# A gated cross-attention and expert kernel: the passage from its first to its second phase rewritten (gates of three tiles on TensorE, twenty slot buffers, loads from one queue)

## The chip, the cores and the metric

The kernel runs on one core of a Trainium2 chip. A core has four engines that compute, each with its own instruction stream executed in order: TensorE (PE, matrix products), VectorE (DVE), ScalarE (ACT) and GpSimd (POOL). SyncE (SP) computes nothing; it issues DMA transfers. ACT and POOL can issue them too, and an engine that has to wait before it issues one holds up everything queued behind it. The metric is the device time of one execution in microseconds (us), as a median of several executions; lower is better.

## The reference

Two gated residual blocks over x of shape (4, 2048, 512), all in float32. The first is cross-attention with 16 heads of 64 to a context of 77 rows per batch; the second is a mixture of 8 experts with a gate over 10 choices (two of them "null"), top 2.

```python
x = x + tanh(g_xattn) * xattn(layernorm(x), ctx, ...)     # attention: q, k, v, softmax, w_out, b_out, tanh(gate)
x = x + tanh(g_ffn)   * ffn(layernorm(x), ...)

def ffn(inputs, gate_w, gate_b, expert_w, expert_b):      # per token
    gate_probs = softmax(x @ gate_w.T + gate_b)           # 10 choices
    weights, selected = top_k(gate_probs, 2)
    true_weights = weights * (selected < 8)
    norm_w = true_weights / denom                         # denom: their sum, or 1
    return sum_k norm_w[k] * (x @ expert_w[selected[k]] + expert_b[selected[k]])
```

## The kernel before

The 8192 tokens are 64 tiles of 128. **Phase 1** goes over the tiles in a software pipeline written out by hand in `step(i)` (line 673): one step computes the attention scores of tile i+1, `attend` (L360: the product of the transposed attention with the folded value and output weights, 20 matmuls) of tile i-1, the residual and the second layer norm of tile i-1, and the gate logits of tile i-2. `attn_move` (L353) turns the attention of a tile by 16 small DMAs from SP. A normed tile is left in one of nine row buffers `rows` (dictionary `hrs`).

The gate logits of a tile (`gate_logits`, L382) are ten products-with-sum on VectorE, one for each choice, against `gwb`, a copy of the gate weights on every partition. `choose` (L410 to L424) takes the two largest, `ratio` (L430) their exponential on ACT, `weigh` (L440 to L445) the weights of the two choices, `place` (L453, TensorE) the running counts, and `dispatch` (L463 to L475) the row numbers, after which POOL scatters the 128 rows to two DRAM arrays `hb[0]` (first choices) and `hb[1]` (second choices), sorted by expert. `place` and `dispatch` take two tiles at a time (m = tile // 2).

**Phase 2** goes over 118 slots of 128 rows, listed in `order`: 16 full blocks that are known early, 35 known after the last tile, 8 partly filled ones, all of first choices; then 51 full and 8 partly filled ones of second choices. A slot n has six parts:

- `slot_load` (L902, L905) reads the start row from a table into a register (L892) and loads the block by five DMAs into a buffer of `ring`. Slots up to 8 are loaded by SP alone; later ones have three of the five DMAs on SP and two on ACT. Partly filled slots are gathered by POOL instead (L881).
- `slot_acc` (L925): POOL gathers the same tokens' rows of the output so far.
- `slot_tr` (L943): the block is transposed on VectorE (partly filled slots: by ACT and TensorE, L952 to L958).
- `slot_pe` (L981): eight matmuls with the expert's weights, into one of six PSUM buffers (`px` and `pe` in turn).
- `slot_out` (L989, L990): VectorE adds the bias, scales, and adds the gathered row.
- `slot_put` (L997): POOL scatters the result to the output.

`first_table`, `second_table` and `part_table` (L831 to L863, VectorE) compute the tables of the slots that depend on all counts.

What sets the order is the program's own text: it is emitted under a manual schedule, so each engine executes its share in the order in which the functions are called. The passage between the phases (L1106 to L1161) is written out: after the last `step`, slots 0 and 1 are multiplied, then tiles 62 and 63 are attended, with the gate logits of 61 and 62 in between and those of 63 spread over the first slots by `tail(q)`. The loop over q from 1 to 118 then runs loads 5 ahead, gathers 3 ahead and transposes 2 ahead. `ring` has 11 buffers: row buffers and pieces of the attention buffers. A load into a buffer waits until the slot that held it has been put.

On the hardware queues of SP and ACT together the program uses eight completion semaphores in rotation: each transfer waits, before it is issued, for the transfer eight before it.

Of the kernel before, what the change touches and what calls it, by code (L numbers as in the profile page):

```python
# [18 lines left out]
P = 128  # L19
# [5 lines left out]
def kernel(  # L25
# [351 lines left out]
    def gate_logits(i, e0, e1):  # L377
        if e0 == 0:
            pgs[i] = stile("pg", i, NG)
        for e in range(e0, e1):  # L380
# [10 lines left out]
            )  # L391


    csum = [small.tile([P, 2, 2, NG], BF16, tag="cs", name="cs_init")]
# [53 lines left out]

    def place(m):

        pps[m] = pp = mm_tile(f"pp{m}")
        for n, (w, v) in enumerate(((upper, msks[m]), (ones_b, counted.pop(m)))):
            nc.tensor.matmul(  # L453
                pp[:, : 4 * NG],
                w,
                v.rearrange("p t k e -> p (t k e)"),
                start=(n == 0),
                stop=(n == 1),
            )

    def dispatch(m):
        pos, pp = poss.pop(m), pps.pop(m)
        nc.vector.tensor_tensor(  # L463
            pos[:, :, :, :NG],
            pp[:, : 4 * NG].rearrange("p (t k e) -> p t k e", t=2, k=2),
            msks.pop(m),
            ALU.mult,
        )
        dst = small.tile([P, 2, 2], I32, tag="dst", name=f"dst_{m}")
        with nc.allow_low_precision("row numbers are whole and below 2^24"):  # L470
            nc.vector.tensor_reduce(dst, pos, AX.X, ALU.add)
        for i in (2 * m, 2 * m + 1):
            hr = hrs.pop(i)
            for k in range(2):
                ins = nc.gpsimd.indirect_dma_start(  # L475
                    out=hb[k],
                    out_offset=bass.IndirectOffsetOnAxis(ap=dst[:, i % 2, k : k + 1], axis=0),
                    in_=hr[:, :].bitcast(I32),
                    in_offset=None,
                    bounds_check=NROWS - 1,  # L480
                    oob_is_err=False,
                )
                tc.declare_no_dep(ins.ins, group="scatter", reason="rows of one bucket differ")
                tc.add_to_no_dep_group("scatter", ins.ins)
                if i > SNAP:
                    tc.declare_no_dep(ins.ins, group="block", reason="blocks full by tile SNAP")
                    tc.add_to_no_dep_group(f"late{i}", ins.ins)

# [184 lines left out]
    def step(i):  # L673
# [14 lines left out]
        if i == NT - 2:  # L688
            slot_tr(0)
            slot_tr(1)  # L690
        if is_tile(i - 1):
# [81 lines left out]
    ]  # L773
    scr = m_flat[:, 6 * D :]
    assert NT * (2 * NE + 1) <= NC * COLS - 6 * D

    def count_rows(cs):
        pc = mm_tile("pc")
# [91 lines left out]
    ]  # L870
    ring += rows[NRB - 3 : NRB - 1]
    px_pool = []
    hss, metas, toks, accs, hsTs, exps, pes, turn = {}, {}, {}, {}, {}, {}, {}, [0, 0]

    def slot_load(n):
# [13 lines left out]
        else:  # L889
            both = n > N1 // 2  # L890
            queues = (nc.sync, nc.scalar) if both else (nc.sync,)
            r = nc.values_load(  # L892
                starts[t][0:1, s : s + 1],
                engines=[ENG.SP, ENG.Activation] if both else [ENG.SP],
                min_val=0,
# [5 lines left out]

            loads = [queues[0].dma_start(hs[:, D:].bitcast(I32), block[:, D:])]  # L902
            for g in range(4):
                loads.append(
                    queues[g // 2 * (len(queues) - 1)].dma_start(  # L905
                        hs[g * 32 : (g + 1) * 32, :D]
                        .rearrange("p (j d) -> p j d", j=4)
                        .bitcast(I32),
                        block[:, g * P : (g + 1) * P].rearrange("(j a) d -> a j d", a=32),
                    )  # L910
                )
# [25 lines left out]
    def slot_tr(n):  # L937
# [11 lines left out]
        ptr = tr_tile(f"str{n}")  # L949
        hp, hsT = (hTs[(turn[1] + k) % len(hTs)] for k in range(2))  # L950
        turn[1] += 2
        nc.scalar.copy(  # L952
# [8 lines left out]
    def slot_pe(n):  # L961
# [13 lines left out]
        hsT = hsTs.pop(n)  # L975
        if n % 2:
            pe = mm_tile(f"pe{n}")
        else:
            pe = px_pool[0].tile([P, 512], F32, tag="px", name=f"px{n}")
# [41 lines left out]
    def rest():  # L1021
# [7 lines left out]
        with tc.If(count > EVER * P):  # L1029
            for n in range(M, len(order)):  # L1030
                for part in (slot_load, slot_acc, slot_tr, slot_pe, slot_out, slot_put):
                    part(n)

    def tail(q):

        i = NT - 1
        if q < 5:
            gate_logits(i, 2 * q, 2 * q + 2)
        elif q == 5:
            choose(i)  # L1040
            ratio(i)
        elif q == 8:
            weigh(i // 2)
            place(i // 2)
            pc = count_rows(csum[0][:, 0])
            dispatch(i // 2)
            first_table(pc)
        elif q == 12:
            second_table()
        elif q == 14:  # L1050
            part_table()

    with tc.manual_schedule():
# [50 lines left out]
        attn_move(1)  # L1104
        nc.sync.dma_start(gwb, gate_w.partition_broadcast(P))
        for i in range(1, NT - 1):  # L1106
            if i == SNAP + 3:
                whole(full[:, 0, :], count_rows(csum[0][:, 0])[:, 0, :])
            if i == NT - 2:
                slot_load(3)  # L1110
                slot_load(4)
            step(i)
            if i == SNAP + 3:
                early_table()
                for n in range(3):
                    slot_load(n)

        phase1.close()
        px_pool.append(ctx.enter_context(tc.tile_pool(name="ps_x", bufs=3, space=PSUM)))
        slot_load(5)  # L1120
        slot_pe(0)
        slot_pe(1)
        slot_tr(2)
        slot_tr(3)
        for i in (NT - 2, NT - 1):
            gate_logits(i - 1, 0, NG)
            attend(i)
            choose(i - 1)
            ratio(i - 1)
            residual(i)  # L1130
            norm_stats(f"h{i}", x1s[i])
            norm_root(f"h{i}")
            if i == NT - 2:
                weigh(i // 2 - 1)
                place(i // 2 - 1)
                dispatch(i // 2 - 1)
            norm_shift(f"h{i}")
            hrs[i] = rows[i % NRB]
            norm_apply(f"h{i}", hrs[i][:, :D], x1s.pop(i))
            if i == NT - 2:  # L1140
                slot_pe(2)
                slot_load(6)
        for n in range(4):
            slot_acc(n)
        tail(0)
        slot_out(0)
        for q in range(1, M + 1):
            if 1 < q < M - 5:
                slot_load(q + 5)
            slot_put(q - 1)  # L1150

            for p in range(max(q, 4), min(q + 4, M)):
                if q == max(p - 3, half if p >= half else 0):
                    slot_acc(p)
# [40 lines left out]
```

## Time and profile before

| | us |
|---|---|
| median of 4 runs (lowest to highest) | 1678.76 (1677.23 to 1681.14) |
| the profiled execution: its own time / its span | 1678.93 / 1677.1 |
| PE busy over the span | 1635.8 (98%) |
| DVE busy | 1293.0 (77%) |
| ACT busy | 884.1 (53%) |
| POOL busy | 469.0 (28%) |
| a slot's eight matmuls when nothing waits | 3.43 |
| `attend` of a tile | 8.6 |

The page cuts the span into 40 slices of 41.9 us; phase 1 ends in the 30th (about 1220 us) and the passage lies in the 30th and 31st. A timeline row gives start, duration, engine, line, what is written and read, and in brackets how long the engine had been idle and whom it waited for. A window row gives a stretch, its length, and busy time with number of instructions for each engine, then the granted clock of TensorE, the DMA share and GB/s. A row of waits gives who waited for whom, the total, how often, and the longest.

### The profile page before, as it was taken

What the parts mean: (1) busy time and instruction counts of PE and PEld (TensorE: products, weight loads), DVE (VectorE), ACT (ScalarE), POOL (GpSimd) and SP (SyncE); (2) the same over time, 40 slices, a digit from 0 to 9 for tenths busy, and PEclk for the clock granted to TensorE, in tenths of its full rate; (3) what the DMA queues carried; (4) which work ended last, traced back from release to release, by engine and by line L of the source; (5) the groups of instructions that cost most, each with busy time, mean ns of one, the idle gap of its engine ahead of it and who ended that gap; (6) DMA issues with size and microseconds to landing.
All of it is one profiled execution on the core that took longest, in us unless ns stands there. A gap on an engine that the chain in (4) does not pass through costs nothing.

```text
span 1677.1 us, 23173 instructions
## 1 busy us (share of the span) xinstructions
PE 1635.8 (98%) x4530; PEld 809.1 (48%) x4530; DVE 1293.0 (77%) x3324; ACT 884.1 (53%) x3188; POOL 469.0 (28%) x617
## 2 busy tenths in 40 slices
PE   8898999999999999999999999999988999999997
PEld 6544445454554545545454554545433444444443
DVE  1554899889898998989989899998988755466653
ACT  2454677767777777777777677776630000100001
POOL 4031111112111111112111121111217656565565
PEclk9999999999999999999999999999998999999999
DMA  7468444336533345534433566766447986688862
GB/s 236 176 195 219 113 93 93 87 96 167 155 86 85 101 100 140 157 88 108 94 94 88 151 167 143 168 139 161 108 109 236 270 239 188 174 252 233 233 188 80
DMA packets 484935, 252.07 MB, mean 150 GB/s; under 512 B 369510, under 2 KB 425830, under 8 KB 484530
## 3 DMA queue, kind: packets, MB, share of 16 engines
q1 hardware_dynamic: 423473, 134.77, 34.3%
q0 software_dynamic: 34528, 103.55, 18.8%
q10 hardware_dynamic: 26784, 12.20, 2.9%
q14 instruction: 110, 0.89, 0.2%
q8 instruction: 40, 0.66, 0.2%
HBM read 119.41 MB, written 100.52 MB: 131 GB/s over the span
## 4 chain that ended last, share of the span: by engine, by line
PE 86%; DVE 4%; DMA 3%; issue 2%; SPq 2%; ACT 1%; POOL 0%; POOLq 0%; DVEq 0%; ACTq 0%
PE po L360 30%; PE sc L281 29%; PE px L981 12%; PE pe L981 11%; DVE prod L382 2%; PE pkv L519 2%; PE xtr L261 2%; SPq L353 1%; PE pv L622 1%; DMA vw_all<-row 1%; DMA gwb<-in_L_ffn_gate_w_dram 1%; DMA acc<-out_dram,row 1%; DMA x<-in_x_dram 0%; PE pm L597 0%; PE str L957 0%
## 5 line engine op out<-in xcount | busy, mean ns | idle before, releaser
L360 PE MATMUL po<-vw,aT 128*128 128x512 f32 (+1 forms) x1280 | 562.8, 595 | 4.0 <-DVE ri L326 3.8
L281 PE MATMUL sc<-m_sb,xnT 128*128 128x385 f32 (+1 forms) x1536 | 552.9, 510 | 0.0
L382 DVE CUSTOM_DVE_ANT_0 prod<-row,gwb,gbias 128x512 f32<-128x512 f32 x640 | 478.0, 747 | 24.5 <-DMA gwb<-in_L_ffn_gate_w_dram 6.6
L360 PEld LDWEIGHTS po<-vw,aT 128*128 128x128 f32 (+1 forms) x1280 | 244.2, 191 | 307.3 <-issue 299.3
L281 PEld LDWEIGHTS sc<-m_sb,xnT 128*128 128x128 f32 x1536 | 283.9, 190 | 212.5 <-issue 86.8
L475 POOL DMA_INDIRECT hb<-row,dst x128 | 128.9, 1007 | 751.1 <-DVE nbh_h L250 672.0
L314 ACT ACTIVATE attn<-sc,nmx 128x77 f32<-128x77 f32 x1024 | 316.0, 347 | 34.4 <-DVE nmx L309 30.6
L314 ACT ACTIVATION_READ_ACCUMULATOR attn<-sc,nmx 128x1 f32 x1024 | 233.2, 228 | 0.0
L981 PE MATMUL px<-big,m_sb 128*128 (+1 forms) x472 | 213.9, 596 | 11.1 <-DVE m_sb L943 10.8
L981 PE MATMUL pe<-big,m_sb 128*128 (+1 forms) x472 | 212.5, 593 | 1.0 <-DVE m_sb L943 1.0
L981 PEld LDWEIGHTS px<-big,m_sb 128*128 128x128 f32 x472 | 89.4, 191 | 121.3 <-issue 108.4
L981 PEld LDWEIGHTS pe<-big,m_sb 128*128 128x128 f32 x472 | 88.8, 190 | 110.1 <-issue 106.9
L303 DVE TENSOR_REDUCE mx<-sc 128x5 f32<-128x385 f32 (+1 forms) x192 | 106.2, 580 | 19.5 <-PE sc L281 17.5
L233 ACT ACTIVATE sdh_h<-mvh_h,eps_t 128x1 f32<-128x1 f32 x64 | 18.9, 295 | 189.9 <-DVE rsa_a L245 180.7
L952 ACT COPY m_sb<-row 128x512 f32<-128x512 f32 x11 | 6.8, 621 | 177.1 <-DMA row<-hb,pidx 174.3
L989 DVE TENSOR_TENSOR yb<-px,blks 128x512 f32<-128x512 f32 x59 | 40.5, 686 | 76.0 <-PE px L981 74.7
L989 DVE TENSOR_TENSOR yb<-pe,blks 128x512 f32<-128x512 f32 x59 | 40.5, 687 | 76.0 <-PE pe L981 75.9
L264 ACT ACTIVATE xnT<-xtr,bet,gam 128x128 f32<-128x128 f32 x256 | 95.4, 452 | 5.3 <-PE xtr L261 5.3
L327 DVE TENSOR_TENSOR attn<-attn,ri 128x1232 f32<-128x1232 f32 x64 | 92.3, 1442 | 5.1 <-DMA aT<-attn 0.8
L373 DVE SCALAR_TENSOR_TENSOR x<-po,gx,x 128x512 f32<-128x512 f32 x64 | 48.0, 750 | 60.7 <-PE pp L453 34.6
L997 POOL DMA_INDIRECT out_dram<-acc,row x75 | 76.3, 1017 | 65.5 <-DVE acc L990 52.7
L336 DVE STREAM_TRANSPOSE attn<-attn 128x1248 f32<-128x1248 f32 x64 | 94.1, 1471 | 0.0
(163 smaller groups left out, 1540.9 us busy)
## 6 DMA issues: line engine op xcount, KB each, us to landing
aT<-attn SPq DMA_DIRECT2D x768, 40.0 KB
x<-in_x_dram SPq DMA_DIRECT2D x64, 256.0 KB
out_dram<-x SPq DMA_DIRECT2D x64, 256.0 KB
aT<-attn SPq DMA_DIRECT2D x256, 36.0 KB
row<-hb SPq DMA_DIRECT2D x138, 64.0 KB
big<-in_L_ffn_expert_w_dram SPq DMA_DIRECT2D x32, 256.0 KB
row<-hb ACTq DMA_DIRECT2D x118, 64.0 KB
vw<-vw_all SPq DMA_DIRECT2D x9, 768.0 KB
```

The source lines that it names most:

```text
L264: nc.scalar.activation(xnT[:, c, :], ptr[:, c, :], AF.Identity, bias=bet[:, c : c + 1], scale=gam[:, c : c + 1],)
L281: nc.tensor.matmul(t[:, : n1 - n0], xnTs[i][:, c, :], m_sb[:, c, n0:n1], start=(c == 0), stop=(c == NC - 1),)
L303: nc.vector.tensor_reduce(mx[:, g0:g1], scs[i, g][:, : (g1 - g0) * SK].rearrange("p (h k) -> p h k", k=SK), AX.X, ALU.max,)
L314: nc.scalar.activation(a[:, h * SK : (h + 1) * SK], t[:, k : k + SK], AF.Exp, bias=nm[:, h : h + 1], scale=SCALE, accum_out=sm[:, h : h + 1],)
L327: nc.vector.tensor_tensor(a, a, ri.unsqueeze(2).to_broadcast([P, H, SK]), ALU.mult)
L336: nc.vector.transpose(a[:, :n], a[:, :n])
L360: nc.tensor.matmul(po, aT[:m, k, :], vw[:m, k, :], start=(k == 0), stop=(k == NKC - 1),)
L382: nc.vector.tensor_tensor_reduce(prod, hrs[i][:, :D], gwb[:, e, :], 1.0, gbias[:, e : e + 1], ALU.mult, ALU.add, pgs[i][:, e : e + 1],)
L475: ins = nc.gpsimd.indirect_dma_start(out=hb[k], out_offset=bass.IndirectOffsetOnAxis(ap=dst[:, i % 2, k : k + 1], axis=0), in_=hr[:, :].bi ...
L981: nc.tensor.matmul(pe, hsT[:, c, :], w[:, c, :], start=(c == 0), stop=(c == NC - 1))
L989: nc.vector.tensor_tensor(tt, pe, b, ALU.add)
L997: ins = nc.gpsimd.indirect_dma_start(out=of, out_offset=bass.IndirectOffsetOnAxis(ap=tok, axis=0), in_=acc, in_offset=None, bounds_check=T ...
```

## The change

Five things are changed, all in the passage and in phase 2, except for a small preparation in phase 1.

1. **Gates of tiles 61, 62 and 63 on TensorE.** The gate weights are loaded once more as ten rows and transposed to `gwT` before step 4 (`setup_gate`). For the three tiles, `gate_transpose` transposes the normed tile (4 transposes, copied to SBUF by ACT), `gate_product` multiplies it with `gwT` (4 products with 10 columns, float32), and one VectorE addition adds the bias. The thirty products-with-sum on VectorE for these tiles are gone.
2. **The slots of the passage stand elsewhere.** Slot loads 3 and 4 are issued after tile 62's output instead of ahead of the last step; loads 3 to 6 stand together there, 7 to 9 after tile 63's output. Slots 1, 2 and 3 are multiplied while tiles 62 and 63 pass their gates; slots 4 and 5 around the product of tile 63's gate; `slot_out` of slots 0 and 1 stands ahead of the choice of tile 63.
3. **The scatter of the last two tiles** is issued one DMA for each of the first four values of q (`later`, `put_rows`), and the tables stand at q = 3, 6 and 9 instead of 8, 12 and 14.
4. **Twenty slot buffers, nine ahead.** `ring` gets nine pieces of `vw` more; loads run 9 ahead, transposes of full slots 4 ahead. All five DMAs of a load are on SP.
5. **Buffers.** Partly filled slots have six transposed-tile buffers of their own (in `gwb`); PSUM buffers go by threes (`n // 3 % 2`) instead of in turn.

```diff
+    def setup_gate():
+        rows10 = rows[NRB - 1][:, :D]
+        ptr = tr_tile("gwtr")
+        for c in range(NC):
+            nc.tensor.transpose(ptr[:, c, :NG], rows10[:NG, c * P : (c + 1) * P], ident[:NG, :NG])
+        nc.vector.tensor_copy(gwT, ptr[:, :, :NG])
+    def gate_transpose(i):
+        ptr = tr_tile(f"gtr{i}")
+        for c in range(NC):
+            nc.tensor.transpose(ptr[:, c, :], hrs[i][:, c * P : (c + 1) * P], ident)
+        nc.scalar.copy(hgT, ptr)
+    def gate_product(i):
+        pl = tr_tile(f"gl{i}")[:, 0, :NG]
+        for c in range(NC):
+            nc.tensor.matmul(pl, hgT[:, c, :], gwT[:, c, :], start=(c == 0), stop=(c == NC - 1))
+        pgs[i] = stile("pg", i, NG)
+        nc.vector.tensor_tensor(pgs[i], pl, gbias, ALU.add)
...
+    ring += [vw_flat[:, v * ROW : (v + 1) * ROW] for v in range(NKC * D // ROW)]
...
-            both = n > N1 // 2
-            queues = (nc.sync, nc.scalar) if both else (nc.sync,)
             r = nc.values_load(
                 starts[t][0:1, s : s + 1],
-                engines=[ENG.SP, ENG.Activation] if both else [ENG.SP],
+                engines=[ENG.SP],
...
-            loads = [queues[0].dma_start(hs[:, D:].bitcast(I32), block[:, D:])]
+            loads = [nc.sync.dma_start(hs[:, D:].bitcast(I32), block[:, D:])]
             for g in range(4):
                 loads.append(
-                    queues[g // 2 * (len(queues) - 1)].dma_start(
+                    nc.sync.dma_start(
...
-        if n % 2:
+        if n // 3 % 2:
             pe = mm_tile(f"pe{n}")
...
     def tail(q):
-        i = NT - 1
-        if q < 5:
-            gate_logits(i, 2 * q, 2 * q + 2)
-        elif q == 5:
-            choose(i)
-            ratio(i)
-        elif q == 8:
-            weigh(i // 2)
-            place(i // 2)
-            pc = count_rows(csum[0][:, 0])
-            dispatch(i // 2)
-            first_table(pc)
-        elif q == 12:
+        if 0 < q <= len(later):
+            put_rows(*later[q - 1])
+        if q == 3:
+            first_table(count_rows(csum[0][:, 0], flat_tr("pclast")))
+        elif q == 6:
             second_table()
-        elif q == 14:
+        elif q == 9:
             part_table()
...
         for i in range(1, NT - 1):
...
-            if i == NT - 2:
-                slot_load(3)
-                slot_load(4)
+            if i == 4:
+                setup_gate()
             step(i)
...
-        slot_load(5)
         slot_pe(0)
-        slot_pe(1)
+        slot_tr(1)
         slot_tr(2)
-        slot_tr(3)
         for i in (NT - 2, NT - 1):
-            gate_logits(i - 1, 0, NG)
             attend(i)
-            choose(i - 1)
-            ratio(i - 1)
+            gate_transpose(i - 1)
             residual(i)
             norm_stats(f"h{i}", x1s[i])
             norm_root(f"h{i}")
-            if i == NT - 2:
-                weigh(i // 2 - 1)
-                place(i // 2 - 1)
-                dispatch(i // 2 - 1)
+            slot_pe(1 if i == NT - 2 else 3)
+            gate_product(i - 1)
             norm_shift(f"h{i}")
             hrs[i] = rows[i % NRB]
             norm_apply(f"h{i}", hrs[i][:, :D], x1s.pop(i))
+            choose(i - 1)
+            ratio(i - 1)
             if i == NT - 2:
+                weigh(i // 2 - 1)
+                place(i // 2 - 1, flat_tr("pp"))
+                dispatch(i // 2 - 1)
                 slot_pe(2)
-                slot_load(6)
+                for n in range(3, 7):
+                    slot_load(n)
+                slot_tr(3)
         for n in range(4):
             slot_acc(n)
-        tail(0)
+        for n in range(7, 10):
+            slot_load(n)
+        gate_transpose(i)
+        slot_tr(4)
+        slot_tr(5)
+        slot_pe(4)
         slot_out(0)
+        slot_put(0)
+        slot_out(1)
+        gate_product(i)
+        choose(i)
+        ratio(i)
+        slot_pe(5)
+        weigh(i // 2)
+        place(i // 2, flat_tr("pplast"))
+        dispatch(i // 2, later)
         for q in range(1, M + 1):
-            if 1 < q < M - 5:
-                slot_load(q + 5)
-            slot_put(q - 1)
+            if q + 9 < M:
+                slot_load(q + 9)
+            if q > 1:
+                slot_put(q - 1)
             for p in range(max(q, 4), min(q + 4, M)):
                 if q == max(p - 3, half if p >= half else 0):
                     slot_acc(p)
-            if 1 < q < M - 2:
-                slot_tr(q + 2)
-            if 2 < q < M:
+            for n, whole_tile in ((q + 4, True), (q + 2, False)):
+                if 5 < n < M and whole_tile == (order[n][1] is not None):
+                    slot_tr(n)
+            if 5 < q < M:
                 slot_pe(q)
-            if q < M:
+            if 1 < q < M:
                 slot_out(q)
             tail(q)
```

More of the change, by code (lines that the diff above doesn't have):

```diff
@@ L391, in gate_logits @@
             )
+    gwT = const.tile([P, NC, NG], F32, name="gwT")
+    def setup_gate():
[15 more added lines that the diff above has]
+        nc.vector.tensor_tensor(pgs[i], pl, gbias, ALU.add)
     csum = [small.tile([P, 2, 2, NG], BF16, tag="cs", name="cs_init")]
@@ L447, in weigh, with place @@
             )
-    def place(m):
-        pps[m] = pp = mm_tile(f"pp{m}")
+    def place(m, pp=None):
+        pps[m] = pp = mm_tile(f"pp{m}") if pp is None else pp
         for n, (w, v) in enumerate(((upper, msks[m]), (ones_b, counted.pop(m)))):
@@ L459, in place, with dispatch @@
             )
-    def dispatch(m):
+    def dispatch(m, later=None):
         pos, pp = poss.pop(m), pps.pop(m)
@@ L474, in dispatch, with put_rows @@
             for k in range(2):
[L475 to L487, printed above, removed]
+                if later is not None:
+                    later.append((hr, dst, i, k))
+                else:
+                    put_rows(hr, dst, i, k)
+    def put_rows(hr, dst, i, k):
+        ins = nc.gpsimd.indirect_dma_start(
+            out=hb[k],
+            out_offset=bass.IndirectOffsetOnAxis(ap=dst[:, i % 2, k : k + 1], axis=0),
+            in_=hr[:, :].bitcast(I32),
+            in_offset=None,
+            bounds_check=NROWS - 1,
+            oob_is_err=False,
+        )
+        tc.declare_no_dep(ins.ins, group="scatter", reason="rows of one bucket differ")
+        tc.add_to_no_dep_group("scatter", ins.ins)
+        if i > SNAP:
+            tc.declare_no_dep(ins.ins, group="block", reason="blocks full by tile SNAP")
+            tc.add_to_no_dep_group(f"late{i}", ins.ins)
     vw_flat = vw.rearrange("p k d -> p (k d)")
@@ L689, in step @@
             slot_tr(0)
-            slot_tr(1)
         if is_tile(i - 1):
@@ L773, with count_rows @@
     ]
[L774 to L778, printed above, removed]
+    hPs = [gwb[:, n, :].rearrange("p (c k) -> p c k", k=P) for n in range(6)]
+    hgT = m_flat[:, 6 * D : 7 * D].rearrange("p (c k) -> p c k", k=P)
+    scr = m_flat[:, 7 * D :]
+    assert NT * (2 * NE + 1) <= NC * COLS - 7 * D
+    def count_rows(cs, pc=None):
+        pc = mm_tile("pc") if pc is None else pc
         nc.tensor.matmul(
@@ L871 @@
     ring += rows[NRB - 3 : NRB - 1]
+    ring += [vw_flat[:, v * ROW : (v + 1) * ROW] for v in range(NKC * D // ROW)]
     px_pool = []
-    hss, metas, toks, accs, hsTs, exps, pes, turn = {}, {}, {}, {}, {}, {}, {}, [0, 0]
+    hss, metas, toks, accs, hsTs, exps, pes, turn = {}, {}, {}, {}, {}, {}, {}, [0, 0, 0]
     def slot_load(n):
@@ L949, in slot_tr @@
         ptr = tr_tile(f"str{n}")
-        hp, hsT = (hTs[(turn[1] + k) % len(hTs)] for k in range(2))
-        turn[1] += 2
+        hp, hsT = (hPs[(turn[2] + k) % len(hPs)] for k in range(2))
+        turn[2] += 2
         nc.scalar.copy(
@@ L1032, in rest, with flat_tr @@
                     part(n)
+    later = []
+    def flat_tr(name):
+        return tr_tile(name).rearrange("p c k -> p (c k)")
     def tail(q):
-        i = NT - 1
-        if q < 5:
-            gate_logits(i, 2 * q, 2 * q + 2)
-        elif q == 5:
-            choose(i)
-            ratio(i)
-        elif q == 8:
-            weigh(i // 2)
-            place(i // 2)
-            pc = count_rows(csum[0][:, 0])
-            dispatch(i // 2)
-            first_table(pc)
-        elif q == 12:
+        if 0 < q <= len(later):
[3 more added lines that the diff above has]
+        elif q == 6:
             second_table()
-        elif q == 14:
+        elif q == 9:
             part_table()
@@ L1105 @@
         nc.sync.dma_start(gwb, gate_w.partition_broadcast(P))
+        nc.sync.dma_start(rows[NRB - 1][:NG, :D], gate_w)
         for i in range(1, NT - 1):
```

## The prediction, made before the changed kernel was run

> **What bounds the kernel now.** I read the page first: its line of busy time and its slices.
>
> ```profile
> span 1677.1 us, 23173 instructions
> PE 1635.8 (98%) x4530; PEld 809.1 (48%) x4530; DVE 1293.0 (77%) x3324; ACT 884.1 (53%) x3188; POOL 469.0 (28%) x617
> ...
> PE   8898999999999999999999999999988999999997
> ...
> PEclk9999999999999999999999999999998999999999
> ```
>
> TensorE is the bound nearly everywhere: 41.3 us of the span are without a matmul, and they lie at the start, at the end and in slices 30 and 31, the passage. Next the windows there (length, then busy time with counts of PE, PEld, DVE, ACT, POOL, then clock, DMA share, GB/s):
>
> ```profile
> 1220.00:1240.00 20.00, 18.90 (x46) 8.26 (x45) 18.29 (x51) 6.04 (x9) 0.00 (x0) 1.00 0.41 81
> 1240.00:1260.00 20.00, 14.39 (x33) 5.81 (x32) 14.37 (x44) 4.79 (x7) 9.27 (x9) 0.93 0.54 154
> 1260.00:1280.00 20.00, 15.62 (x33) 6.96 (x34) 18.42 (x40) 1.58 (x2) 14.76 (x15) 0.82 0.76 226
> 1280.00:1300.00 20.00, 19.03 (x48) 8.27 (x47) 16.60 (x41) 0.00 (x0) 13.99 (x14) 1.00 0.79 246
> ```
>
> Then PE's timeline for the stretches that it waited:
>
> ```profile
> 1237.91 0.18 PE L453 MATMUL pp<-msk,upper 128*128 128x40 bf16 x1 [0.79 <-DVE msk L412]
> ...
> 1238.43 3.69 PE L981 MATMUL px<-big,m_sb 128*128 x8 [0.32 <-issue]
> 1242.35 8.82 PE L360 MATMUL po<-vw,aT 128*128 128x512 f32 x20 [0.22 <-DMA aT<-attn]
> ...
> 1264.38 5.12 PE L981 MATMUL px<-big,m_sb 128*128 x8 [9.78 <-DVE m_sb L943]
> ...
> 1291.23 3.67 PE L981 MATMUL pe<-big,m_sb 128*128 x8 [0.97 <-DVE m_sb L943]
> ```
>
> From 1221.5 (slot 0) to 1294.7 (end of slot 11) PE needs 12 x 3.43 for slots and 2 x 8.6 for tiles 62 and 63, 58.4 us; it takes 73.2. The 14.8 us are the five waits (12.1), 1.7 of lower clock in the slot after the long wait (5.12 against 3.43), and about 1 of small steps. The long wait is for VectorE's transpose of slot 4. From 1300 to 1660 PE waits once more, 0.99 us at 1471.17 for a transpose. What VectorE did instead of that transpose stands in its timeline and in the page's groups:
>
> ```profile
> 1255.98 0.69 DVE L989 TENSOR_TENSOR yb<-px,blks 128x512 f32<-128x512 f32 x1
> 1259.17 0.75 DVE L990 SCALAR_TENSOR_TENSOR acc<-yb,row,acc 128x512 f32<-128x512 f32 x1 [2.51 <-DMA acc<-out_dram,row]
> ...
> 1261.49 0.75 DVE L990 SCALAR_TENSOR_TENSOR acc<-yb,row,acc 128x512 f32<-128x512 f32 x1 [0.84 <-DMA acc<-out_dram,row]
> ```
> ```profile
> L382 DVE CUSTOM_DVE_ANT_0 prod<-row,gwb,gbias 128x512 f32<-128x512 f32 x640 | 478.0, 747 | 24.5 <-DMA gwb<-in_L_ffn_gate_w_dram 6.6
> ```
>
> Gate logits of 62 ran from 1242.1 to 1250.0; outputs of slots 0 and 1 waited for POOL's gathers; the transpose of slot 4 came at 1263.6. Last, SP's timeline, for what a load costs it when it issues all five DMAs:
>
> ```profile
> 1203.14 0.37 SPq L902 DMA_DIRECT2D row<-hb  x1
> 1203.70 1.89 SPq L905 DMA_DIRECT2D row<-hb  x4
> 1206.23 0.35 SPq L902 DMA_DIRECT2D row<-hb  x1
> 1206.77 1.84 SPq L905 DMA_DIRECT2D row<-hb  x4
> 1209.19 0.35 SPq L902 DMA_DIRECT2D row<-hb  x1
> ...
> 1267.76 11.29 SPq L905 DMA_DIRECT2D row<-hb  x2
> ```
>
> A load takes SP 3.0 us (3.09, 2.96). The last row is SP held 10.5 us (the list of waits) for an earlier load's transfer; ACT, which issues two of each load's five, stood waiting for the choice of tile 63 at the time.
>
> **The change part by part.**
>
> *Gates, VectorE.* Thirty products at a pitch of 0.79 us (1229.3 to 1237.1 for ten), 23.8 us, leave VectorE in the passage; three additions of about 0.15 come. This is not the gain itself: only what PE waited for counts.
>
> *Gates, TensorE.* Four float32 transposes take 0.44 us (the input transposes on the chain). The product: four calls, two passes each as in all float32 products here, so eight weight loads and eight tiny matmuls. No row shows one with 10 columns. Below: the pitch of the transposes, 0.11 each, 0.9 us. Above: eight weight loads end to end at 0.19, 1.5. I take 1.1, eight times the 0.141 of a transpose's weight load, the nearest row. Three tiles: 3 x (0.44 + 1.1) = 4.6 us, all on PE's path, 4.0 to 5.8. [...] ACT's copies (0.62) and the DMA of ten rows hide behind matmuls; ACT has 5 us busy of 20 there.
>
> *Preparation before step 4.* Four transposes of ten rows, at most 0.44 us, PE being full there; the VectorE copy, about 0.15, comes while PE runs scores. I take 0.4, from 0.1 to 0.5.
>
> *Slots and tiles, followed through.* From 1221.5, with the durations above: slot 0 to 1224.9; `attend` 62 to 1233.5 (its sixteen moves end at 1223.2 on SP and landed within 2 us); transposes and slot 1 to 1237.4; product to 1238.5. Then addition, two norm steps (0.33) and choice (0.65) on VectorE, and PE waits for the mask until 1239.8: 1.25 us, plus 0.45 to the next slot, as in the row at 1238.43. Slot 2 to 1243.7, `attend` 63 to 1252.3. SP's moves for it no longer have loads 3 and 4 ahead and end near 1237.5. Transposes of 62, slot 3, product: 1257.3. VectorE's norm steps of 63 stand behind the addition that awaits this product; ACT's norm (0.81) follows, so tile 63 can be transposed at 1258.8: 1.5 us of waiting. Slot 4 to 1262.7, product of 63 to 1263.8, slot 5 to 1267.3. Meanwhile outputs 0 and 1 wait for gathers: before, the first was issued 3.7 us after tile 63's `attend` and landed 4.2 later, the second 2.3 later again; now 1262.1, and the choice needs them only by 1265.6. `place` is queued behind slot 5, `dispatch` on VectorE behind `place`, the transpose of slot 6 behind both: PE waits 1.3. Then two outputs at 1.36, transposes at 0.64 and the first table, 4.2 us (1285.98 to 1290.2 before), stand ahead of slot 8's transpose: PE waits 1.4. The second table (4.5) ahead of slot 11's: 0.6. Slot 11 ends at 1291.2 instead of 1294.7. Check: 14.8 less 4.6 added, less 6.5 of new waits, is 3.7; I take **3.5**. If every product costs 1.5, 1.2 less (the chain runs through all three); if 0.9, 0.6 more. If the choice is faster and the waits halve, about 3 more. No new wait is long enough for the clock: after 0.97 us the slot took 3.67, after 9.78 it took 5.12.
>
> *Moved loads and scatters.* Loads 3 to 6 run on SP from 1238.3 to 1250.4, before tile 63's output; load 3 is wanted by 1252. Loads 7 to 15 run from 1253.9 at 3.0 each; slot 7's transpose is at 1270, slot 8's at 1276. Behind a waiting load stand only loads. On POOL the first late scatter waits for `dispatch` (1267.5), and put 1, gather 5 and the next scatters stand behind it: at 1.3 us an issue, gather 5 lands about 1275 and is wanted at 1279; gather 6 about 1279, wanted 1281. The tables' rows are needed by load 16 (scatters landed about 1284, slot 16's transpose near 1298). So nothing here, while these margins of 2 to 14 us hold.
>
> *Steady part.* PE is at 20.00 of 20.00 in the windows from 1300 to 1360, and whole to 1450, so twenty buffers and nine ahead gain nothing there. At 1471, where second choices start, gathers must wait for all puts; with transposes four ahead and loads that no longer wait for slots eleven back, 0.99 us goes. Partly filled slots' POOL loads now start four slots earlier; POOL can fall about 7 us behind there, against the same amount of slack, and six PSUM buffers lie between it and PE. I take **1.0**, from -1 to 1.
>
> Sum against the profiled execution's own 1678.93 (1.8 above its span, 0.17 above the median): 3.5 + 1.0 - 0.4 = 4.1, so 1674.8; as a median **1674.7**.
>
> **The rivals.**
>
> [...]
>
> *The waits move, and little is left (no change).* Outputs 0 and 1 stand ahead of the last choice; past 1265.6 every us of a late gather delays the choice, the scatter, slot 6 and both tables. A gather landing 3 us late beyond that margin, or products at 1.5 with waits of 8 instead of 6.5, leave 0.5 to 2: 1677. For it: VectorE already waited 2.51 and 0.84 for these gathers. Against: the gathers start no later relative to `attend`.
>
> *The waits vanish (faster).* If choice and tables hide behind slots, 14.8 + 1.0 - 5.0 leaves 10 at most; half of the new waits gone gives 1671.
>
> **How the numbers follow.** Forecast (1672.5 to 1677) 0.50, little left 0.27, waits vanish 0.10, SP behind 0.08, some other stall that loses more than 0.2% 0.05. A measurement of this kernel tells about 0.2%, 3.4 us, from no change: 1675.4 is the line. Four fifths of the forecast, the vanishing waits and a little of "little left" lie below: 0.52 faster. Slower: SP, the other stall, and 0.04 of "little left", 0.17. Same: 0.31. The range leaves out SP's case and the outermost gains: 1670.5 to 1679.5.
>
> **What would show it.** PE: no wait above 2 us between 1221 and 1300, slots after it at full clock, slot 11 ending near 1291. VectorE: no L382 row after tile 60's; its longest waits for gathers and for `place`. The product's eight matmuls in 0.9 to 1.5 us. SP's load rows at 3.0 us, its waits then for puts, not for loads; PE whole from 1300 on, with nothing where second choices begin. Wrong it would be if PE waited for transposes after 1300 (SP or POOL late), if VectorE waited beyond 1266 for gather 1, or if transposing tile 63 waited much longer than 1.5 us.

## The result and the profile after

The changed kernel takes 1676.17 us in the median of 36 runs (1673.73 to 1680.22), against 1679.48 for the kernel before in the same comparison (56 runs, 1676.52 to 1684.25): a ratio of 0.998 with a 95% interval from 0.9976 to 0.9985. That is 3.3 us less, 2.5 to 4.0 by the interval. The forecast was 1674.7, or 4.1 us less. The total came out nearly right; the parts of the sum did not. The prediction put the line for a gain that can be told from none at 1675.4, and the median lies just above it; with this many runs the interval leaves out no change all the same.

The page after the change (span, busy time, PE's and the clock's slices, the gate row):

```profile
span 1674.0 us, 23024 instructions
...
PE 1640.9 (98%) x4570; PEld 813.5 (49%) x4570; DVE 1271.0 (76%) x3268; ACT 885.3 (53%) x3191; POOL 468.5 (28%) x617
...
PE   8898999999999999999999999999999999999997
...
PEclk9999999999999999999999999999999999999999
...
L382 DVE CUSTOM_DVE_ANT_0 prod<-row,gwb,gbias 128x512 f32<-128x512 f32 x610 | 455.4, 747 | 22.6 <-DMA gwb<-in_L_ffn_gate_w_dram 7.3
```

The thirty products-with-sum are gone (x610 where it was x640). PE does 5.1 us more and the two weak slices are filled. The windows of the passage, in the same columns as before:

```profile
1220.00:1240.00 20.00, 18.55 (x54) 8.74 (x53) 9.11 (x24) 8.07 (x11) 0.00 (x0) 1.00 0.34 71
1240.00:1260.00 20.00, 18.63 (x52) 8.92 (x51) 5.68 (x22) 4.30 (x7) 6.56 (x8) 0.91 0.49 139
1260.00:1280.00 20.00, 17.56 (x45) 7.90 (x45) 14.92 (x42) 1.46 (x4) 11.51 (x12) 0.91 0.79 220
1280.00:1300.00 20.00, 19.98 (x47) 8.66 (x46) 18.71 (x39) 0.00 (x0) 15.72 (x15) 1.00 0.89 263
```

VectorE is relieved (5.68 busy in the second window instead of 14.37) and PE is busy, but its clock is 0.91 in two windows. PE's timeline says where:

```profile
1236.57 0.96 PE L412 MATMUL gl<-gwT,m_sb 128*128 128x10 f32 x8
1238.62 0.19 PE L476 MATMUL pp<-msk,upper 128*128 128x40 bf16 x1 [1.09 <-DVE msk L435]
...
1239.14 5.39 PE L1012 MATMUL px<-big,m_sb 128*128 x8 [0.30 <-issue]
...
1256.83 0.96 PE L412 MATMUL gl<-gwT,m_sb 128*128 128x10 f32 x8
1259.15 0.66 PE L406 MATMUL gtr<-ident,row 128*128 128x128 f32 x4 [1.37 <-ACT row L255]
1259.80 5.40 PE L1012 MATMUL pe<-big,m_sb 128*128 x8
...
1270.78 7.13 PE L1012 MATMUL px<-big,m_sb 128*128 x16 [1.20 <-DVE m_sb L974]
...
1279.16 3.70 PE L1012 MATMUL px<-big,m_sb 128*128 x8 [1.24 <-DVE m_sb L974]
```

The waits stand where the prediction put them and are about as long. But slots 2 and 4 take 5.39 and 5.40 us instead of 3.6 to 3.7: 1.7 us each, at a lowered clock.

Starts of slots in the profiled executions, before and after, give the account. From slot 0 to slot 12 the passage takes 73.2 before and 72.9 after: in this execution it gave 0.3, not 3.5. From slot 12 to the last matmul it is 372.5 and 371.1: 1.4 gained. The step with `setup_gate` is 0.4 longer. That makes 1.3 us. What else separates the two spans lies ahead of tile 2 (1.6 us; the other profiles differ there from that of the kernel before by up to 1.6 either way) and behind the last matmul (0.3). The median gain is larger, 3.3; the experiments show what can make it so.

From 1300 on PE waits for nothing; windows of 100, 100, 100 and 50 us:

```profile
1300.00:1400.00 100.00, 100.00 (x234) 44.27 (x233) 62.46 (x93) 0.00 (x0) 68.06 (x66) 1.00 0.87 251
1400.00:1500.00 100.00, 100.00 (x258) 45.87 (x257) 52.85 (x77) 8.93 (x16) 67.94 (x65) 1.00 0.79 223
1500.00:1600.00 100.00, 100.00 (x234) 44.27 (x233) 60.30 (x89) 0.00 (x0) 59.11 (x59) 1.00 0.74 219
1600.00:1650.00 50.00, 50.00 (x138) 23.37 (x137) 23.28 (x34) 7.27 (x13) 38.22 (x36) 1.00 0.51 160
```

### The profile page after: what moved, and what is told of

The parts are those of the page before. It is cut to its first block, busy times and chain, and to the rows that moved or that the text cites. A ratio compares the mean times of both kernels' runs of the same rounds, so it can differ in the third digit from the quotient of the medians.

```text
span 1674.0 us, 23024 instructions
## 1 busy us (share of the span) xinstructions
PE 1640.9 (98%) x4570; PEld 813.5 (49%) x4570; DVE 1271.0 (76%) x3268; ACT 885.3 (53%) x3191; POOL 468.5 (28%) x617
## 4 chain that ended last, share of the span: by engine, by line
PE 91%; DVE 2%; DMA 2%; SPq 2%; ACT 1%; issue 1%; POOL 0%; POOLq 0%; DVEq 0%; ACTq 0%
PE po L360 31%; PE sc L281 30%; PE px L1012 12%; PE pe L1012 11%; PE pv L651 2%; PE pkv L548 2%; PE xtr L261 2%; DMA vw_all<-row 1%; DVE prod L382 1%; SPq L936 1%; SPq L353 1%; DMA gwb<-in_L_ffn_gate_w_dram 1%; DMA x<-in_x_dram 0%; PE pm L626 0%; PE str L988 0%
## 5 line engine op out<-in xcount | busy, mean ns | idle before, releaser
L382 DVE CUSTOM_DVE_ANT_0 prod<-row,gwb,gbias 128x512 f32<-128x512 f32 x610 | 455.4, 747 | 22.6 <-DMA gwb<-in_L_ffn_gate_w_dram 7.3
L1012 PE MATMUL px<-big,m_sb 128*128 x424 | 187.9, 597 | 2.7 <-DVE m_sb L974 2.4
L1012 PE MATMUL pe<-big,m_sb 128*128 x392 | 173.5, 598 | 0.0
L1012 PEld LDWEIGHTS px<-big,m_sb 128*128 128x128 f32 x424 | 80.5, 191 | 102.4 <-issue 98.4
L1012 PEld LDWEIGHTS pe<-big,m_sb 128*128 128x128 f32 x392 | 74.7, 191 | 94.0 <-issue 91.5
L255 ACT ACTIVATE row<-x,nbh_h,rsh_h 128x512 f32<-128x512 f32 x64 | 52.1, 814 | 64.2 <-DVE nbh_h L250 64.2
```

Of the source, the lines that this page charges most:

```text
L382: nc.vector.tensor_tensor_reduce(prod, hrs[i][:, :D], gwb[:, e, :], 1.0, gbias[:, e : e + 1], ALU.mult, ALU.add, pgs[i][:, e : e + 1],)
L1012: nc.tensor.matmul(pe, hsT[:, c, :], w[:, c, :], start=(c == 0), stop=(c == NC - 1))
```

## The experiments

**The gates of the three tiles back on VectorE**, in the new order.

```diff
     def gate_transpose(i):
-        ptr = tr_tile(f"gtr{i}")
-        for c in range(NC):
-            nc.tensor.transpose(ptr[:, c, :], hrs[i][:, c * P : (c + 1) * P], ident)
-        nc.scalar.copy(hgT, ptr)
+        return
     def gate_product(i):
-        pl = tr_tile(f"gl{i}")[:, 0, :NG]
-        for c in range(NC):
-            nc.tensor.matmul(pl, hgT[:, c, :], gwT[:, c, :], start=(c == 0), stop=(c == NC - 1))
-        pgs[i] = stile("pg", i, NG)
-        nc.vector.tensor_tensor(pgs[i], pl, gbias, ALU.add)
+        gate_logits(i, 0, NG)
...
-            if i == 4:
-                setup_gate()
```

> The changed kernel with the gates of tiles 61 to 63 back on VectorE, ten products each at the places where the TensorE products stood; all else as changed. If the gates are the part that pays, each tile's 7.9 us stands in the chain that TensorE waits for: some 4 us more at the counts, 5 at slot 4, 5 at slot 6, and more dips of the clock, less 3.8 us of TensorE work: 1683 to 1690, slower than before. If the reordering alone made the gain, the time stays near 1676.

Measured: 1689.93 (4 runs), ratio 1.006 (1.0044 to 1.0075). The waits of PE (who for whom, total, times, longest):

```profile
PE pe L1005 <- DVE m_sb L967: 8.6, 1, 8.6
PE pp L469 <- DVE msk L428: 7.5, 1, 7.5
PE pplast L469 <- DVE msk L428: 2.2, 1, 2.2
PE px L1005 <- DVE m_sb L967: 2.2, 1, 2.2
```

From slot 0 to slot 12 it is 87.9 us, 15 more than with the gates on TensorE. The new order without the new gates is slower than the kernel before: it puts `place` and the slots right behind the choices, and pays only if a choice comes soon after its tile. The reverse, the new gates in the old order, was not run, so what the gates alone would have gained is not known.

**The ring left at eleven buffers**, loads still nine ahead and transposes four ahead.

```diff
-    ring += [vw_flat[:, v * ROW : (v + 1) * ROW] for v in range(NKC * D // ROW)]
```

> The changed kernel with the ring left at eleven buffers; loads still stand nine ahead and transposes of full slots four ahead, but a load again waits for the slot eleven back. If the twenty buffers are what took away the wait of 0.99 us where second choices begin, that wait is back and the time is about 1 us above the changed kernel (1677); if the transposes four ahead did it, the wait stays away and the time is the changed kernel's, 1676. The passage is the same in both: slots 2 and 4 after the gate products at the lower clock again, 5.4 us, if that dip belongs to the order of the passage and not to the one execution seen so far.

Measured: 1676.35 (11 runs), ratio 0.9979 (0.997 to 0.9987), the same as the whole change. PE waits for nothing where second choices begin. So the buffers are not what removed that wait. SP waits in their stead, with no one waiting for SP; its longest row between 1300 and 1660:

```profile
SPq L932 <- DMA out_dram<-acc,row: 32.5, 2, 31.7
```

Something else in this run tells more. From the start of its gate product to slot 2 it is 2.78 us, where the changed kernel has 2.57, and yet slot 2 was not slowed:

```profile
1239.85 0.96 PE L412 MATMUL gl<-gwT,m_sb 128*128 128x10 f32 x8
1241.90 0.19 PE L476 MATMUL pp<-msk,upper 128*128 128x40 bf16 x1 [1.10 <-DVE msk L435]
...
1242.63 3.69 PE L1011 MATMUL px<-big,m_sb 128*128 x8 [0.51 <-issue]
...
1261.60 5.29 PE L1011 MATMUL pe<-big,m_sb 128*128 x8
```

The passage took 71.4 here, 1.5 less than in the changed kernel's profiled execution.

**Two queues for the later loads**, as before the change: ACT issues two of the five DMAs from slot 9 on.

```diff
+            both = n > N1 // 2
+            queues = (nc.sync, nc.scalar) if both else (nc.sync,)
...
-                engines=[ENG.SP],
+                engines=[ENG.SP, ENG.Activation] if both else [ENG.SP],
...
-                    nc.sync.dma_start(
+                    queues[g // 2 * (len(queues) - 1)].dma_start(
```

> The changed kernel with three of a load's five transfers on SP and two on ACT from slot 9 on, as before. If loading from SP alone only frees ACT and costs nothing, because TensorE is full from 1300 us on either way, the time is that of the changed kernel within 1 us (1675 to 1677) with no wait of TensorE after 1300 us. If the single queue is what gave the gain (ACT no longer holding SP's transfers), it is slower by 2 us or more, with SP waiting for a load's transfer near the choice of tile 63 as in the kernel before.

Measured: 1675.37 (12 runs), ratio 0.9979 (0.997 to 0.9987). PE has the same waits and none after 1300. Who issues the loads makes no difference here that the intervals (about 1.5 us either way) could show.

**Transposes of full slots two ahead** from slot 34 on, instead of four.

```diff
-            for n, whole_tile in ((q + 4, True), (q + 2, False)):
+            ahead_by = 4 if q < 30 else 2 if q > 31 else -q
+            for n, whole_tile in ((q + ahead_by, True), (q + 2, False)):
```

> The changed kernel with transposes of full slots four ahead only up to slot 33 and two ahead, as before, from slot 34 on; twenty buffers and loads nine ahead stay. If the transposes four ahead took away the wait where second choices begin, a wait of about 1 us for a transpose is back near slot 62, and the stretch from slot 59 to slot 64 takes 18.3 us instead of 17.2. If the buffers or the earlier loads did it, the stretch takes 17.2.

Measured in one execution: 1675.34. PE's row at slot 62:

```profile
1467.72 3.70 PE L1012 MATMUL px<-big,m_sb 128*128 x8 [0.45 <-DVE m_sb L974]
```

From slot 59 to slot 64 it is 17.9 us; before the change it was 18.4, after it 17.2. So transposes four ahead are worth 0.7 of the 1.2 us there. The run with eleven buffers and the run with two queues take 17.2 as well, so the other 0.5 are neither the buffers nor the single queue; the loads' distance, the PSUM order and the partly filled slots' own buffers were not tried alone.

**Unread matmuls in two pauses**: two products of two passes each, full size, 1.8 us, ahead of `place` for tiles 60 and 61 and ahead of tile 63's transposes on PE (between the product of tile 62's gate and slot 4).

```diff
+    def filler(name, calls):
+        t = flat_tr(name)
+        for _ in range(calls):
+            nc.tensor.matmul(t, ident, we[:, 0, 0, :], start=True, stop=True)
...
+                filler("fill61", 2)
                 weigh(i // 2 - 1)
...
+        filler("fill62", 2)
         gate_transpose(i)
```

> The changed kernel with two unused full-size products (four matmuls of 512 columns, 1.7 us) on TensorE in the wait for tile 61's mask and again in the wait for tile 63's norm; their result is read by nobody. If the dips come from TensorE having nearly 3 us without full-size matmuls, slots 2 and 4 take 3.6 us: 3.6 us won, about 1 us lost to fillers longer than the waits, 1673 to 1674. If the dips have another cause, the two slots still take 5.4 us and the time is about 1 us above the changed kernel, 1677.

Measured: 1673.14 (5 runs), ratio 0.9967 (0.9954 to 0.998). PE's timeline:

```profile
1237.96 1.96 PE L1073 MATMUL fill<-big,ident 128*128 128x512 f32 x4
...
1239.82 3.68 PE L1012 MATMUL px<-big,m_sb 128*128 x8
...
1258.84 3.62 PE L1012 MATMUL pe<-big,m_sb 128*128 x8
```

Slots 2 and 4 take 3.68 and 3.62 us instead of 5.39 and 5.40, and the passage takes 69.6 us instead of 72.9. Work that nobody needs, put where PE waited, makes the passage shorter. (For the whole time the interval just overlaps that of the changed kernel, which begins at 0.9976; the slots' rows leave no doubt.) With the pauses filled these two slots were not slowed, so in the changed kernel it was the pause that lowered the clock, not the slots' own data or buffers.

**The slots between a product and what waits for it**: slot 2 ahead of `place`, slot 4 ahead of tile 63's transposes, slot 5 between these and tile 63's gate product, slot 6 ahead of the last `place`, with transposes five ahead.

```diff
+                slot_pe(2)
                 weigh(i // 2 - 1)
                 place(i // 2 - 1, flat_tr("pp"))
                 dispatch(i // 2 - 1)
-                slot_pe(2)
...
-        gate_transpose(i)
-        slot_tr(4)
-        slot_tr(5)
+        slot_tr(6)
         slot_pe(4)
+        gate_transpose(i)
...
         slot_put(0)
+        slot_tr(7)
+        slot_pe(5)
         slot_out(1)
...
-        slot_pe(5)
+        slot_pe(6)
         weigh(i // 2)
```

> The changed kernel with slots put between a gate product and what waits for it: slot 2 ahead of the counts of tiles 60 and 61, slot 4 ahead of the transposes of tile 63, slot 6 ahead of the counts of tiles 62 and 63; transposes of full slots one earlier. Nothing is added or left out. If the four waits of 1.1 to 1.4 us and the two slots at lower clock (5.4 us instead of 3.6) are what ate the gain, TensorE's waits fall from 5.2 us to about 2 (a wait for slot 9's transpose behind the first table), both dips go, and slot 12 starts about 8 us after less time: 1668 to 1671. If the dips come from something else (the small matmuls themselves, or the moment), two slots still take 5.4 us and the gain is about 3: 1672 to 1674.

Measured: 1670.29 (6 runs), ratio 0.9948 (0.9936 to 0.996). One wait is left in the passage, and it too is followed by a slow slot (slot 9, the first of the three in this row, took 5.24 from start to start):

```profile
1277.27 12.26 PE L1012 MATMUL pe<-big,m_sb 128*128 x24 [2.03 <-DVE m_sb L974]
```

VectorE was at the first table then (1272.0 to 1276.5), as the prediction's steps had it for slot 8. From slot 0 to 12 it is 67.2 us.

**The same order with every gate product done six times**, so that PE has no pause but 4.9 us of matmuls with 10 columns.

```diff
-        for c in range(NC):
-            nc.tensor.matmul(pl, hgT[:, c, :], gwT[:, c, :], start=(c == 0), stop=(c == NC - 1))
+        for _ in range(6):
+            for c in range(NC):
+                nc.tensor.matmul(pl, hgT[:, c, :], gwT[:, c, :], start=(c == 0), stop=(c == NC - 1))
```

> The kernel with slots put between a gate product and what waits for it, with each gate product computed six times over into the same place (4.9 us of 10-column matmuls back to back, no wait), which adds 12 us and shows what TensorE's clock does after busy but small matmuls. If small matmuls count as idle for the clock, the slots behind them (2, 4 and 6) take 5 us or more instead of 3.6. If only time without any matmul counts, they take 3.6 to 3.7.

Measured in one execution: 1693.22. PE's timeline at tile 61, and windows of 3.41 us there (the last three numbers are clock, DMA share, GB/s):

```profile
1237.53 7.20 PE L413 MATMUL gl<-gwT,m_sb 128*128 128x10 f32 x48
1244.57 5.23 PE L1013 MATMUL px<-big,m_sb 128*128 x8
```
```profile
1237.47:1240.88 3.41, 3.41 (x32) 3.35 (x30) 0.00 (x0) 0.00 (x0) 0.00 (x0) 1.00 0.43 112
1240.88:1244.29 3.41, 3.41 (x18) 3.41 (x17) 0.00 (x0) 0.00 (x0) 0.00 (x0) 0.50 0.37 87
1244.29:1247.71 3.42, 3.42 (x7) 1.77 (x7) 1.10 (x9) 2.39 (x3) 0.00 (x0) 0.50 0.41 98
1247.71:1251.12 3.41, 3.41 (x11) 1.43 (x10) 2.18 (x10) 0.00 (x0) 0.00 (x0) 1.00 0.42 98
```

PE is busy for 3.41 of 3.41 us in the first window, and its clock is 0.50 all the same in the next two. Slots 2, 4 and 6 take 5.23, 6.15 and 5.38 us. In this run the matmuls with 10 columns counted as a pause. By that a product of 0.81 us, the wait of 1.1 behind it and what lies around `place` acted as one pause of 2.6 in the changed kernel. (The kernel lost 23 us against the run with the slots between, not the 12 expected: the lowered clock stretched the first two of the small products too, to 7.20 and 7.94 us, where the third, at 1.00 to 1285.25, took 5.42.)

**The tables one to two slots later**, on top of the slots between.

```diff
-        if q == 3:
+        if q == 4:
...
-        elif q == 6:
+        elif q == 8:
             second_table()
-        elif q == 9:
+        elif q == 11:
             part_table()
```

> The kernel with slots put between a gate product and what waits for it, and the three tables one to two slots later (q = 4, 8, 11), so that slot 9's transpose stands ahead of the first table on VectorE. Nothing is left out. That kernel still waited 2.03 us for slot 9's transpose, and slot 9 then took 5.24 us. If such gaps are all that is left in the passage, both go, TensorE has no wait over 0.5 us from slot 0 to slot 13, slots 0 to 12 take 63.5 us instead of 67.2, and the median is 3 to 4 us below 1670.3: about 1666.5. If the tables only push the wait on to another slot (12 or 14), the gain is under 2 us.

Measured: 1671.17 (5 runs), ratio 0.9948 (0.9934 to 0.9961), no gain over the run with the slots between. The wait for slot 9 went, as expected (0.5 is left at slot 10), and slots 0 to 12 took 63.9 us; a new wait came at slot 14:

```profile
1297.05 3.40 PE L1012 MATMUL px<-big,m_sb 128*128 x4 [2.42 <-DVE m_sb L974]
```

Ahead of it VectorE had stood 1.48 and 2.59 us at slot outputs (the profile names no one whom it waited for) and then run the second table, and POOL had been issuing back to back since 1271, a scatter of tile 62 or 63, a put and a gather for each slot, 3.9 to 4.4 us for 3.43 of matmuls:

```profile
1279.35 0.99 POOL L504 DMA_INDIRECT hb<-row,dst  x1 [0.31 <-issue]
1280.64 0.98 POOL L1028 DMA_INDIRECT out_dram<-acc,row  x1 [0.30 <-DVE m_sb L974]
1281.93 1.05 POOL L956 DMA_INDIRECT acc<-out_dram,attn  x1 [0.30 <-issue]
1283.28 1.50 POOL L504 DMA_INDIRECT hb<-row,dst  x1 [0.30 <-issue]
```

**The late scatters behind every second slot**, on top of that.

```diff
-        if 0 < q <= len(later):
-            put_rows(*later[q - 1])
+        if q % 2 == 0 and 0 < q <= 2 * len(later):
+            put_rows(*later[q // 2 - 1])
```

> The order of the run with the slots between, the tables at slots 4, 8 and 11 as in the run before it, and now the four late scatters of the last pair issued behind every second slot (2, 4, 6, 8) instead of one behind each of slots 1 to 4. In the run with the later tables POOL issued three indirect transfers a slot back to back from 1271 to 1287, about 4.3 us for a slot of 3.43, and DVE then stood at 1286.6 and 1291.1 for gathers, until TensorE stood 2.42 us at slot 14. If POOL's row of transfers is what held that stretch, the 2.42 us go, and slots 12 to 20 take 27.5 us instead of 31.8: about 1667 in the median. If the second table's 5 us on DVE are what held it, the wait stays near 2 us, and the time stays at 1671.

Measured: 1668.49 (5 runs), ratio 0.9934 (0.992 to 0.9947): by the ratio 11 us (9 to 13) faster than the kernel before. Slots 12 to 20 take 27.5 us where they took 31.8, and PE's one wait from 1150 on is

```profile
PE pe L1012 <- DVE m_sb L974: 0.5, 1, 0.5
```

VectorE no longer stands at slot outputs there, although the second table is where it was. POOL's row of transfers was what held that stretch.

**Unread matmuls ahead of slot 9**, on top of the slots between, with the tables where the change put them.

```diff
+            if q == 9:
+                filler("fill9", 2)
             if 6 < q < M:
                 slot_pe(q)
```

> The order of the run with the slots between, with the tables where they were, and four full-size matmuls that nobody reads (1.8 us) ahead of slot 9, in the 2.03 us that TensorE waits for slot 9's transpose there. If the clock is lowered by the time without full-size matmuls, slot 9 takes 3.43 to 3.7 instead of 5.24, and the time is about 1668.7 against 1670.3. If it is not, slot 9 stays at 5.2 and the time at 1670.3 or above.

Measured: 1669.48 (5 runs), ratio 0.994 (0.9927 to 0.9954). PE's timeline:

```profile
1275.55 1.88 PE L1073 MATMUL fill<-big,ident 128*128 128x512 f32 x4
1277.75 10.57 PE L1012 MATMUL pe<-big,m_sb 128*128 x24 [0.32 <-DVE m_sb L974]
```

Slot 9, the first of the three in the last row, takes 3.53 us from start to start instead of 5.24, and slots 0 to 12 take 65.6 instead of 67.2. The medians differ by less than their intervals; the profiles show the step.

## Why the prediction was right in sum and wrong in its parts

The near hit is in part luck. The sum left out a loss, the clock's, of 1.7 us for each slow slot; products that cost less than it took (0.9) and a steady part that gave more (0.4) paid for some of it, and waits that cost more (0.7) added to it. Without a slow slot these terms turn the 4.1 us into 4.7, with one into 3.0, with two into 1.3. Of the signs that the prediction named, no wait of PE above 2 us and PE whole from 1300 on came; full clock behind the waits, a product within 0.9 to 1.5 us and slot 11 ending near 1291 (it ended at 1293.3) did not.

*What bounded the kernel before.* The reading holds but for one size: 1.7 us for the slot after the long wait compares a row of 5.12, which includes the end of its last matmul, with a pace of 3.43. From start to start that slot took 4.95, so the clock cost 1.5 and the small steps 1.2. The sum of 14.8 stays.

*Gates, VectorE.* Right that the thirty products matter only through PE's waits; with them back, PE waits 20.8 us in the passage.

*Gates, TensorE.* Over-sized. I took 1.1 us for a product, between 0.9 and 1.5; it takes 0.81 from its start to that of the slot behind it (1265.03 to 1265.84; 1238.60 to 1239.41 in the run with the slots between), below my lower end. Eight weight loads, one every 0.11 us (seven of them make a row of 0.86 us at 1265.04), with small matmuls beneath them are all there is. Three tiles: 0.9 us better than the sum.

*Preparation before step 4.* 0.4 predicted, 0.39 measured.

*The new waits.* Right in place and nearly in size: 1.25 and 0.45 predicted for the mask and the slot behind it, 1.09 and 0.30 shown; 1.5 for the norm of 63, 1.37 shown; 1.3 and 1.4 for slots 6 and 8, 1.20 and 1.24 shown; 0.6 for slot 11, not shown. Their idle time sums to 5.2 instead of 6.5. From start to start, with the first matmul behind each wait also later, they cost about 7.2, so 0.7 more than the sum had.

*The clock.* This is the step that failed: "No new wait is long enough for the clock: after 0.97 us the slot took 3.67, after 9.78 it took 5.12." It looked at each wait alone. What counted in these runs is the time without full-size matmuls (1.96 us of it in a stretch of 3.41 kept the clock, 2.10 lost it, as the last section has it), and in that the tiny products are pause like the wait. (Whether the transposes are too, these runs don't tell: counted either way, they leave the stretches read that kept the clock apart from those that lost it.) Ahead of slot 2 that is 0.81 + 1.09 and what lies around `place`, 2.57 us from the end of slot 1 to the start of slot 2; ahead of slot 4 it is 2.97. Both slots lost 1.7. The account of the profiled execution closes with it, though the term for the waits was itself taken from this execution: the forecast of 69.7 for the passage, less 0.9 for the products, plus 0.7 for the waits, plus 3.45 for the clock, is 72.95; it took 72.91.

Why the median gained more than this execution's passage: the loss comes and goes. In the passage the clock was lowered for stretches of 3.41 us or whole multiples of that (10.24 in the kernel before), and the two in the changed kernel's profile begin six times 3.41 apart (1240.24 and 1260.72). The stretches in question are these, one before and one in each slow slot:

```profile
1236.83:1240.24 3.41, 2.02 (x12) 1.35 (x12) 1.07 (x8) 2.18 (x3) 0.00 (x0) 1.00 0.44 120
1240.24:1243.66 3.42, 3.42 (x6) 1.37 (x5) 2.01 (x9) 0.21 (x1) 0.90 (x1) 0.50 0.44 93
...
1257.31:1260.72 3.41, 2.04 (x11) 1.28 (x11) 2.76 (x11) 2.40 (x4) 2.71 (x3) 1.00 0.67 152
1260.72:1264.14 3.42, 3.42 (x5) 1.35 (x4) 2.39 (x4) 0.46 (x1) 2.73 (x4) 0.50 0.96 281
```

In the run with eleven buffers the pause ahead of slot 2 (1239.85 to 1242.63) was cut by an edge of the grid:

```profile
1237.53:1240.95 3.42, 3.28 (x14) 1.81 (x12) 0.48 (x4) 1.27 (x2) 0.00 (x0) 1.00 0.35 57
1240.95:1244.35 3.40, 1.94 (x6) 0.98 (x7) 1.49 (x12) 2.39 (x3) 0.00 (x0) 1.00 0.45 127
...
1258.01:1261.42 3.41, 2.04 (x14) 1.47 (x12) 1.66 (x9) 1.32 (x2) 2.08 (x2) 1.00 0.52 135
1261.42:1264.84 3.42, 3.42 (x6) 1.51 (x5) 2.89 (x6) 1.54 (x3) 2.79 (x3) 0.50 0.91 237
```

1.1 us of the pause lies in one stretch and 1.7 in the next, and the clock stays at slot 2. Of the four profiled executions with the change's own order in the passage, two had two slow slots (the change itself, and the one with two queues) and two had one (eleven buffers, transposes two ahead). With two, the profile's account gives a gain of 1.3; with one, 3.0; with none, 4.7. The measured 3.3 lies among them. The mean granted clock of each timed run bears this out: one lowered stretch takes 0.001 off it (half of 3.41 in 1674), and the 14 runs at 0.996 have a median of 1674.9, the 12 at 0.995 one of 1676.9 and the 7 at 0.994 one of 1677.2. But stretches near the start and the end of the program count in that mean as well (0.50 from 147.98 to 151.39 and from 1666.91 on in the changed kernel's profile), and the kernel before has a single profile; so how often slots 2 and 4 are slow, and how much of the 3.3 that explains, is argued and not shown.

*Moved loads and scatters.* Nothing, as costed. Output 1 waited 0.64 us for its gather, and the choice of tile 63 stood waiting for its product until 1266.0, not for a gather. But the margin on POOL was thin: in the shorter passage of the run with the later tables it was gone.

*Steady part.* 1.0 predicted, 1.4 measured, nearly all at slot 62. The reason was half right: transposes four ahead carry 0.7 of it, the buffers none, and the rest is open.

*The rivals.* For SP falling behind, the 0.08 of the prediction, there is no support: no run shows loads from SP alone landing later. A load takes SP 3.0 us, PE waits for nothing from 1300 to 1650, and with two queues the time is the same (1675.37). "The waits vanish" at 1671 is what the order of the text can still give: with the slots between it is 1670.3, and with tables and scatters moved as well 1668.5. "Little left", 1677, had the right size for an execution with two slow slots, by another cause than the two that it named.

## What to carry to other kernels

When a kernel is bound by TensorE, add up the time without full-size matmuls, small products included, before asking whether a wait is short enough: here 2.10 us of it within one stretch of 3.41 was followed by a clock of 0.50 in the next, and slot 9 took 5.24 us, where it took 3.53 with the pause filled. Work that is ready belongs between a small product and the thing that waits for its result, and if there is none, even an unread matmul shortened the passage here. After each such step look at the next queue: once PE no longer waited there, VectorE's tables (2.03 us of waiting at slot 9) and then POOL's row of three transfers a slot (2.42 at slot 14) set the pace.

## What the runs showed of the hardware that was not expected

- The clock was granted in stretches of 3.41 us on a grid that lay differently against the program's steps in each execution: an edge came 1.10 us behind the start of slot 2 in the changed kernel (1240.24, 1239.14) and 1.68 ahead of it in the run with eleven buffers (1240.95, 1242.63). In the five profiles whose passage was read by stretches (before, after, eleven buffers, slots between, six gate products) the lowered stretches read are 3.41, 6.83 (six gate products, 1240.88 to 1247.71) or 10.24 us long (before, 1257.03 to 1267.27). Over the stretches read that were at full clock, I summed the time from the end of one full-size matmul to the start of the next. With each matmul counted as 0.43 us, its pace, the clock stayed up to 1.96 us in a stretch (six gate products, slot 5 to 1281.84), and from 2.10 us on (slots between, ahead of slot 9) the next stretch had half the clock; nothing lies between, and there is no exception among them. With the matmuls' ends as the profile models them the two figures are 1.80 and 1.99.
- In the run with six gate products a stretch that PE spent on 10-column matmuls from 1237.53 to its end at 1240.88, busy for 3.41 of 3.41 us, was followed by two at a clock of 0.50; in the run with the slots between a stretch with 1.42 of 3.41 us busy (1275.28 to 1278.69) was followed by one.
- In a float32 product with 10 columns the weight loads and the matmuls both came every 0.11 us, two for each call (eight from 1265.03 to 1265.84 in the changed kernel). In the run with six gate products 33 matmuls, nearly all of them these, fall into a stretch at full clock (1281.84 to 1285.25) and 18 into one at 0.50 (1240.88 to 1244.29).
